# Mamba-2 block plus mixture of LoRA experts: B, half of h and the sums of squares turned by VectorE and DRAM instead of TensorE, with urgencies set unit by unit

## The chip, the cores and the metric

The kernel runs on one core of one Trainium2 chip. The metric is the device time of one execution in microseconds. Before the change the median of three runs is 1601.93 us (1601.57 to 1602.46). PE is TensorE's matmul, PEld its weight load, DVE VectorE, ACT ScalarE, POOL GpSimd, SP the engine that issues the DMAs.

## The reference

One token sequence of S = 1024 with 512 features is normalized, goes through a state-space layer (128 heads of 64 channels, state size 128, 8 groups, chunks of 128 tokens) and through a feed-forward part with routed low-rank experts, and both are added to the input. What matters here, cut:

```python
proj = jnp.einsum('bsd,ed->bse', x, in_proj_w)          # gate, h | B | C, dt
xc = jax.lax.conv_general_dilated(xc, conv_w, (1,), [(K - 1, 0)], ...)   # 4 taps per channel
hBC = jax.nn.silu(jnp.transpose(xc + conv_b, (0, 2, 1)))
...
xch = (hs * dt[..., None]).reshape(b, nc, CHUNK, H, P)
Y_diag = jnp.einsum('bzlhn,bzshn,bhzls,bzshp->bzlhp', Cc, Bc, L, xch)
states = jnp.einsum('bzlhn,bhzl,bzlhp->bzhpn', Bc, decay_states, xch)
Y_off = jnp.einsum('bzlhn,bzhpn,bhzl->bzlhp', Cc, prev, jnp.exp(A_cum))
Y = (Y_diag + Y_off).reshape(b, s, H, P) + hs * D[None, None, :, None]
g = y * jax.nn.silu(gate)
gg = g.reshape(b, s, G, INTER // G)
gg = gg * jax.lax.rsqrt(jnp.mean(gg * gg, axis=-1, keepdims=True) + EPS)
return jnp.einsum('bsi,oi->bso', gg.reshape(b, s, INTER) * norm_w, out_proj_w)
```

The convolution and the gate are computed with channels on the partitions and time along the free dimension. The sums over time (`states`, `Y_diag`) need h and B with time on the partitions, and the mean of squares needs a sum over channels for each time step. These are the places where data is turned.

## The kernel before

The inner 8192 channels are 64 blocks of 128 (two heads each); two blocks make a unit u of 0 to 31, four units make a group g of 0 to 7. All fp32 products are split into a high and a low fp32r part and done as three matmuls (hi x hi, hi x lo, lo x hi).

The kernel does not emit instructions as it goes. Each piece of work is registered with `op(engine, cost, function, reads, writes, urge=...)`, and `Plan.run` is a list scheduler. It goes through time with the costs written at the call sites, and on each engine starts the ready piece with the smallest urgency for which a buffer is free. For PE it adds a price from `URGE` when the shape of matmul changes: `SHORT` (transposes, cb), `LONG` (512 columns), `HALVES` (64 weight columns: yo and y), `MIDDLE` (ps). The result is a fixed order on each engine; on the chip every engine works through its order and waits on semaphores where data is not there. An `op` on SP that is a DMA has a `lag`, the time the plan allows until landing. `CAPS` bounds the buffers of each kind; buffers come from shared pools (`big`, `wide`, `small`, and `banks`, the 8 banks of PSUM).

The stages:

- Start: x is loaded in 8 parts, normalized, transposed on PE (`xT`) and split into `xh`, `xl`, both [features, time]. The time steps dt are projected and their cumulative sums go to DRAM (`acum_d`, `exp_d`), from where they are broadcast back as `L` and `e`.
- For each group, `group` makes B and C by `block`, the turned B as `bh` and `bl` (high and low part, time on the partitions), and `cbm`, the masked product of C and B. The turn before is 8 PE transposes into two PSUM banks (L718), read by ACT for `bh` (L720) and by DVE for `bl` (L722).
- `block` (L662 on) projects 128 channels: 2 x 12 matmuls of 512 columns into two banks (`pp_r`, L426), and for h, B and C the four taps of the convolution: one on ACT (L685), three on DVE (L694), then SiLU on ACT (L697).
- `scan(u, hs, gate)` does a unit: `L` (decays: ReLU and Exp on ACT, product with `cbm` on DVE, L762); `hT`, 8 PE transposes of h per block into PSUM (L776); `xdt`, turned h times dt, by two DVE instructions from PSUM (L778); `xf` on POOL, `xdh` on ACT and `xdl` on POOL; `ps`, the states' products (L802) and `st`, their recurrence on DVE; `yo` and `y` (L837, L849), their evacuations `tt` and `yt` on DVE, and the gated result on POOL, stored to DRAM (`g_d`).
- The feed-forward part (`ffn`) comes near the end of the scan.
- The output projection: for each group and each chunk z of 128 time steps `gr` is loaded from `g_d`, split into `gh` and `gl`, squared (ACT) and reduced over the group's 8 blocks into `sq` (DVE, L911), and 24 matmuls `po` (L920) run. For each four chunks PE transposes `sq` into `vp` (L932), DVE reduces it to one sum per time step (L934), and the reciprocal root scales `po` into `acc` (L941).

Of the kernel before, what the change touches and what calls it, by code (L numbers as in the profile page):

```python
# [49 lines left out]
URGE = dict(w=9.24, part=-0.279, proj=-0.002, evac=-1.876, silu=-2.632, group=-0.486, hT=0.407, xdt=2.385, xf=-1.176,  # L50
            split=-0.323, ps=-2.368, st=-1.089, Ll=-7.231, Lr=6.458, Le=2.863, Lm=5.964, el=-2.393, yo=0.086,
            tt=-1.918, y=3.42, yt=-3.901, out=1.039, switch=2.019, short=0.042, long=0.133, halves=-1.335,
            middle=-3.841, leave=2.869, c0=36.517, c=0.019, ffn=32.348, rt=-5.457, la=-0.436, early=-6.249,
            hold=0.232, gate=-0.092, w0=79.012)
CAPS = dict(hs=5, gate=15, ct=2, L=7, e=2, xdt=25, wr=3, wh=3, wl=8, y=4, tt=2, xf=2, mm=13, ts=3, yy=17)
# [42 lines left out]
class Plan:  # L98
# [33 lines left out]
    def run(self):  # L132
# [11 lines left out]
        while left:  # L144
            began = False
            soon = 1e30
            for e in ENGINES:
# [4 lines left out]
                for o in todo[e]:  # L152
                    same = e == "PE" and o.mode == mode == HALVES
                    if o.ready > t + 1e-9:
                        soon = min(soon, o.ready)
                        stay |= same and o.ready < t + URGE["hold"]
                        continue
# [3 lines left out]
                    if e == "PE" and o.mode != mode:  # L161
                        urge += URGE[("short", "long", "halves", "middle")[o.mode]]
                        if mode == HALVES:
                            urge += URGE["leave"]
# [10 lines left out]
                    for k, bs in wanted.items():  # L175
                        pool = k.pool
                        many[pool] = many.get(pool, 0) + len(bs)
                        if k.live + len(bs) > k.cap or (k.fifo and bs[0].order != k.given):
                            good = False
                            break  # L180
                        if k.late and pool.spare() < many[pool]:
                            good = False
                            break
                        ready = sorted(f[0] for f in pool.free)
                        if len(ready) < many[pool]:
                            good = False
                            break
                        if ready[many[pool] - 1] > t + 1e-9:
                            soon = min(soon, ready[many[pool] - 1])
                            stay |= same and ready[many[pool] - 1] < t + URGE["hold"]  # L190
                            good = False
                            break
# [50 lines left out]
def block_kernel(ctx, tc, x, in_w, conv_w, conv_b, dt_bias, A_log, Dv, norm_w, out_w,  # L243
# [30 lines left out]
    elast_d = dram.tile([H, NZ], F32, name="elast_d")  # L274
    g_d = [dram.tile([BPG, P, S], F32, name=f"g_d{g}") for g in range(G)]
# [5 lines left out]
    big, wide, small = Pool("big", 30, 1024, sb), Pool("wide", 3, 1792, sb), Pool("small", 15, 512, sb)  # L281
    K = {n: Kind(big, CAPS.get(n, 1)) for n in ("hs", "gate", "bT", "ct", "cbm", "bh", "bl", "L", "e", "xdt", "dts", "As",
# [6 lines left out]
    K |= {n: Kind(small, c, late=True) for n, c in dict(acc=8, sq=2, ow_r=4, moe=1, lb=1).items()}  # L289
# [11 lines left out]
    def thing(name):  # L301
        return pl.buf(None, name)

# [13 lines left out]
    XH, XL = new("xh", "xh", S, FR), new("xl", "xl", S, FR)  # L317
    G_D = [thing(f"g_d{g}") for g in range(G)]

    def dma(dst, src, lag, **kw):  # L320
        return op("SP", 0.45, lambda: sp.dma_start(dst(), src()), lag=lag, **kw)
# [15 lines left out]
    op("PE", 6.0, warm_up(12), w=[warm], urge=-9.0)  # L337
# [5 lines left out]
    for n, what in enumerate((0, 1, wdt, 2, 3, w0, 4, 5, 6, 7)):  # L343
        lag, urge = 2.64 + (0.3, 0.38)[n > 2] * n + 0.1 * (n > 2), -8.0 + 0.001 * n
        if what in (wdt, w0):
            dma(what[0], lambda row=144 if what is wdt else 0: in_w[row], lag, w=[what[0]], urge=urge)
        else:
            j, i = divmod(what, 2)
            dma(lambda j=j, i=i: xts[j]()[:, i, :], lambda z=what: x[zsl(z), :], lag, w=[(xts[j], 1 << i)], urge=urge)

    def load(*pairs):
# [5 lines left out]
    op("SP", 1.0, load((dtb, dt_bias), (negA, A_log)), w=[(CONST, 1)], urge=-7.9, lag=5.0)  # L357
    op("SP", 3.5, load((cw, conv_w), (cb, conv_b), (nw, norm_w), *(
        (Dt[64 * j:64 * j + 64, :], Dv[j:j + 1, :].partition_broadcast(64)) for j in range(2))), w=[(CONST, 2)],
       urge=2.5, lag=6.0)  # L360
    split(*wdt, -7.3)
# [45 lines left out]
    def project(w, acc, half, urge, take=(), quarters=False):  # L407

        for q in range(2) if quarters else ():
            def go(q=q):  # L410
                n, c = 0, slice(q * 256, q * 256 + 256)
                hi, lo = w[0](), w[1]()
                for a, b in ((hi, XH()), (hi, XL()), (lo, XH())):
                    for k in range(NK):
                        pe.matmul(acc()[:, c], a[:, k, :], b[:, k, halves(half)][:, c], start=n == 0, stop=n == 11)
                        n += 1
            mk = 3 << 4 * half + 2 * q
            op("PE", 1.44, go, r=[w[0], w[1], (XH, mk), (XL, mk)], w=[(acc, 1 << q)], urge=urge,
               take=take if q == 0 else (), mode=LONG)
# [244 lines left out]
    def block(u, i, row, ci, kind, name):  # L664
# [3 lines left out]
        if row:  # L668
            dma(raw, lambda: in_w[row], 3.6, w=[raw], urge=urge + URGE["w"])
# [35 lines left out]

    def group(g, u):
        gr = groups[g]
        urge = u + 0.16 + URGE["group"]
# [3 lines left out]
        for hf in range(2):  # L712
            zs = slice(hf * 4, hf * 4 + 4)
            acc = new("mm", f"bt{g}_{hf}", P)

            def turn(acc=acc, hf=hf):
                for z4 in range(4):
                    pe.transpose(acc()[:, z4, :], gr.B()[:, zsl(hf * 4 + z4)], ident)  # L718
            op("PE", 0.436, turn, r=[gr.B], w=[acc], urge=urge, take=[gr.bh, gr.bl] if not hf else ())
            op("ACT", 0.49, lambda acc=acc, zs=zs: act.activation(gr.bh()[:, zs, :], acc(), AF.Copy), r=[acc],  # L720
               w=[(gr.bh, zmask(hf))], urge=urge)
            op("DVE", 0.6, lambda acc=acc, zs=zs: dve.tensor_tensor(  # L722
                gr.bl()[:, zs, :], acc(), f32(gr.bh()[:, zs, :]), ALU.subtract), r=[acc, (gr.bh, zmask(hf))],
                w=[(gr.bl, zmask(hf))], urge=urge)
# [12 lines left out]


    def scan(u, hs, gate):
        g, gr = u // 4, groups[u // 4]  # L740

        def at(what):
            return u + URGE[what]
# [20 lines left out]
        for j in range(2):  # L764
            b = 2 * u + j
            cols = slice(j * P, (j + 1) * P)
            for hf in range(2):
                tp = new("ts", f"hT{b}_{hf}", P)
# [3 lines left out]
                late = 0.02 * (2 * j + hf)  # L772

                def turn(tp=tp, hf=hf, j=j):
                    for z4 in range(4):
                        pe.transpose(tp()[:, z4, :], hs[j]()[:, zsl(hf * 4 + z4)], ident)  # L776
                op("PE", 0.436, turn, r=[hs[j]], w=[tp], urge=at("hT") + late, take=[xdt[j]] if not hf else ())
                op("DVE", 0.6, lambda tp=tp, j=j, b=b, zs4=zs4: dve.tensor_tensor(  # L778
                    xdt[j]()[:, zs4, :].rearrange("p z (a c) -> p z a c", a=2),
                    tp().rearrange("p z (a c) -> p z a c", a=2),  # L780
                    dts()[:, zs4, 2 * b:2 * b + 2].unsqueeze(3).to_broadcast([P, 4, 2, 64]), ALU.mult),
                    r=[tp, dts], w=[(xdt[j], mk)], urge=at("xdt") + late)
# [11 lines left out]
        for i in range(4):  # L794
# [20 lines left out]
            op("DVE", sum(0.45 if z == 0 else 0.77 for z in zz), steps, r=[pt, eA], w=[(st, mk & 255)],  # L815
               urge=at("st") + 0.02 * i)
        for j in range(2):
# [6 lines left out]
            for hf in range(2):  # L824
                late = 0.04 * (2 * j + hf)
# [5 lines left out]
                def off(yo=yo, hf=hf, j=j):  # L831
# [7 lines left out]
                op("PE", 0.218 * n, off, r=[(st, 0x78 if hf else 7), gr.C], w=[yo], urge=at("yo") + late, take=[tt],  # L839
                   mode=HALVES)  # L840
# [4 lines left out]
                def diag(yp=yp, hf=hf, j=j):  # L845
# [6 lines left out]
                   urge=at("y") + late, take=[yt], mode=HALVES)  # L852
# [12 lines left out]
    def gates(u, base):  # L865
        return [block(base + URGE["gate"], 2 + j, 2 * u + j, None, "gate", f"g{2 * u + j}") for j in range(2)]

    first = [gates(u, URGE["early"] + 0.3 * u) for u in range(2)]
    for u in range(NU):
        if u % 4 == 0:  # L870
            group(u // 4, u)
        hs = [block(u, j, 64 + 2 * u + j, 2 * u + j, "hs", f"h{2 * u + j}") for j in range(2)]
# [6 lines left out]
    crs = ctile([P, 72], "crs")  # L879
    for g in range(G):  # L880
# [18 lines left out]
        for z in range(NZ):  # L899
# [24 lines left out]
            if z % many == many - 1:  # L924
                vp = new("ts", f"vp{g}_{z}", P)
                first = z - many + 1
                rs = crs[:, g * NZ + first:g * NZ + z + 1]
                RS = thing(f"rs{g}_{z}")

                def sums(vp=vp, sq=sq, many=many):  # L930
                    for j in range(many):
                        pe.transpose(vp()[:, j, :], sq()[:, j, :], ident)  # L932
                op("PE", 0.109 * many, sums, r=[sq], w=[vp], urge=urge + URGE["c"] - 0.1)
                op("DVE", 0.1 + 0.13 * many, lambda vp=vp, rs=rs, many=many: dve.tensor_reduce(  # L934
                    rs, vp()[:, 0:many, :], AX.X, ALU.add), r=[vp], w=[RS], urge=urge)
# [55 lines left out]
```

## Time and profile before

| what | value |
|---|---|
| median of three runs | 1601.93 us |
| the profiled execution | 1604.36 us |
| its span | 1602.7 us, 28828 instructions, granted TensorE clock 0.998 |
| VectorE, ScalarE and GpSimd busy | 1282.2, 1294.4 and 832.9 us |
| DMA | 229.98 MB, mean 143 GB/s |
| transposes of h / B / sums on PE | 512 / 64 / 64, 272 to 279 ns each (they overlap) |
| table loads on ACT | 203 by the instruction order, 1283 ns each |

The scan with its projections takes the time up to about 1240 us, and the output projection the rest. A group of instructions carries its line, its engine, its operation, its tile, the shapes, the count, the busy time in us, the mean duration in ns and the idle time of the engine just before. Matmul durations overlap, so spacing of starts tells more than duration.

### The profile page before, as it was taken

How to read it: one execution, taken by the hardware profiler on the slowest of the kernel's cores; microseconds unless marked ns; L12 is line 12 of the kernel's file. 1: busy time of each engine (PE TensorE's matmuls, PEld its weight loads, DVE VectorE, ACT ScalarE, POOL GpSimd, SP SyncE). 2: the span in 40 equal slices, each digit the busy share in tenths (PEclk: the TensorE clock that was granted, in tenths of full speed). 3: DMA queues.
4: the chain of work that ended last, by engine and by line, in shares of the span. 5: the costliest groups of instructions: out<-in, count | busy, mean ns of one | idle time of the engine just before them, and what ended most of it. 6: DMA issues, size and time to landing. Idle time of an engine off the chain costs nothing.

```text
span 1602.7 us, 28828 instructions
## 1 busy us (share of the span) xinstructions
PE 1592.1 (99%) x10616; PEld 1355.2 (85%) x10616; DVE 1282.2 (80%) x2209; ACT 1294.4 (81%) x2275; POOL 832.9 (52%) x768
## 2 busy tenths in 40 slices
PE   8999999999999999999999999999999999999999
PEld 8888888888888888888888888888887888888887
DVE  6798987786888788777878877787788788888874
ACT  6899989997999899799989988998973554444531
POOL 3269757847775776678576847866755000000000
PEclk9999999999999999999999999999999999999999
DMA  4534725444443555344344615544545655554512
GB/s 132 186 105 155 244 89 175 136 136 135 148 154 117 172 158 162 108 161 155 116 138 146 204 66 157 183 155 129 155 135 173 169 139 156 158 142 127 138 55 72
DMA packets 140605, 229.98 MB, mean 143 GB/s; under 512 B 11056, under 2 KB 76720, under 8 KB 140464
## 3 DMA queue, kind: packets, MB, share of 16 engines
q1 hardware_dynamic: 140464, 228.14, 46.5%
q8 instruction: 84, 1.38, 0.4%
q14 instruction: 57, 0.47, 0.1%
HBM read 191.39 MB, written 36.70 MB: 142 GB/s over the span
## 4 chain that ended last, share of the span: by engine, by line
PE 93%; POOL 3%; ACT 2%; issue 1%; DMA 0%; DVE 0%; SPq 0%; POOLq 0%; DVEq 0%
PE pp_r L426 45%; PE po L920 22%; PE y L849 7%; PE yo L837 6%; PE ps L802 5%; PE hT L776 3%; PE pf L652 1%; PE cb L732 1%; POOL yt L856 1%; POOL xdl L791 1%; POOL xf L784 1%; ACT L L758 1%; POOL g L859 1%; PE bt L718 0%; PE vp L932 0%
## 5 line engine op out<-in xcount | busy, mean ns | idle before, releaser
L426 PE MATMUL pp_r<-xh,wh 128*128 128x512 f32 x1144 | 454.2, 397 | 0.0
L426 PE MATMUL pp_r<-xh,wl 128*128 128x512 f32 x1144 | 446.3, 390 | 1.3 <-POOL wl L325 1.3
L426 PE MATMUL pp_r<-xl,wh 128*128 128x512 f32 x1144 | 446.4, 390 | 0.0
L694 DVE SCALAR_TENSOR_TENSOR h<-pp_r,cw,h 128x512 f32<-128x512 f32 (+2 forms) x384 | 283.3, 748 | 73.7 <-ACT h L685 67.7
L758 ACT ACTIVATE L<-L,As 128x128 f32<-128x128 f32 x1024 | 319.4, 391 | 0.0
L325 POOL TENSOR_TENSOR wl<-wr,wh 128x512 fp32r<-128x512 f32 x144 | 192.4, 1340 | 208.3 <-ACT wh L324 182.8
L426 PEld LDWEIGHTS pp_r<-xh,wl 128*128 128x128 f32 x1144 | 214.8, 188 | 48.3 <-POOL wl L325 2.2
L426 PEld LDWEIGHTS pp_r<-xh,wh 128*128 128x128 f32 x1144 | 215.0, 188 | 45.7 <-issue 3.9
L426 PEld LDWEIGHTS pp_r<-xl,wh 128*128 128x128 f32 x1144 | 215.2, 188 | 41.0
L762 DVE TENSOR_TENSOR L<-L,cbm 128x1024 f32<-128x1024 f32 x128 | 189.0, 1493 | 52.5 <-ACT L L760 52.1
L910 ACT ACTIVATE gr<-gr 128x1024 f32<-128x1024 f32 x64 | 67.8, 1060 | 157.6 <-DVE gl L908 157.6
L856 POOL TENSOR_TENSOR yt<-yt,tt 128x384 f32<-128x384 f32 (+1 forms) x128 | 157.3, 1240 | 68.8 <-DVE yt L853 60.4
L859 POOL TENSOR_TENSOR g<-yt,g 128x512 f32<-128x512 f32 x128 | 185.2, 1458 | 3.1
L791 POOL TENSOR_TENSOR xdl<-xf,xdh 128x512 fp32r<-128x512 f32 (+1 forms) x128 | 152.3, 1198 | 28.1 <-ACT xdh L789 28.1
L784 POOL TENSOR_TENSOR xf<-xdt,dec 128x512 f32<-128x512 f32 (+1 forms) x128 | 131.8, 1040 | 55.8 <-DVE xdt L778 55.6
L813 DVE SCALAR_TENSOR_TENSOR st<-st,eA,ps 128x64 f32<-128x64 f32 x768 | 151.4, 276 | 1.1
L911 DVE TENSOR_REDUCE sq<-gr 128x128 f32<-128x1024 f32 x64 | 128.7, 2013 | 19.1 <-ACT gr L910 19.0
L760 ACT ACTIVATE L<-L 128x1024 f32<-128x1024 f32 x128 | 135.6, 1059 | 1.5
L920 PE MATMUL po<-owh,gh 128*128 128x512 f32 x512 | 128.9, 394 | 0.0
L778 DVE TENSOR_TENSOR xdt<-hT,dts 128x512 f32<-128x512 f32 x128 | 80.2, 683 | 59.7 <-PE hT L776 59.7
L920 PE MATMUL po<-owh,gl 128*128 128x512 f32 x512 | 126.5, 389 | 0.0
L920 PE MATMUL po<-owl,gh 128*128 128x512 f32 x512 | 126.5, 389 | 0.0
(175 smaller groups left out, 2806.1 us busy)
## 6 DMA issues: line engine op xcount, KB each, us to landing
L<-acum_d SPq DMA_DIRECT2D x128, 512.0 KB, 5.8
wr<-in_w SPq DMA_DIRECT2D x144, 256.0 KB, 2.8
g_d<-g SPq DMA_DIRECT2D x64, 512.0 KB, 4.6
gr<-g_d SPq DMA_DIRECT2D x64, 512.0 KB, 6.7
e<-exp_d SPq DMA_DIRECT2D x128, 224.0 KB, 6.3
ow<-out_w SPq DMA_DIRECT2D x64, 256.0 KB, 3.6
x<-x SPq DMA_DIRECT2D x8, 256.0 KB, 5.3
acc<-x SPq DMA_DIRECT2D x8, 256.0 KB, 4.3
```

Source lines behind the costliest of these rows:

```text
L325: op("POOL", dur[1], lambda: pool.tensor_tensor(lo(), raw(), f32(hi()), ALU.subtract), r=[raw, hi], w=[lo], urge=urge, port=True)
L426: pe.matmul(acc(), a[:, k, :], b[:, k, halves(half)], start=n == 0, stop=n == 11)
L694: dve.scalar_tensor_tensor(d, acc()[:, :n], cw[:, ci, k:k + 1], d, ALU.mult, ALU.add)
L758: act.activation(L()[:, z, :], L()[:, z, :], AF.Relu, bias=As()[:, z, h:h + 1], scale=-1.0)
L760: op("ACT", 0.97, lambda L=L: act.activation(L(), L(), AF.Exp, scale=-1.0), w=[L], urge=at("Le") + 0.05 * a, table="exp")
L762: op("DVE", 1.14, lambda L=L: dve.tensor_tensor(L(), L(), gr.cbm(), ALU.mult), r=[gr.cbm], w=[L], urge=at("Lm") + 0.05 * a, port=True)
L784: op("POOL", 1.0 if n == 4 else 0.8, lambda xf=xf, j=j, b=b, zs=zs, n=n: pool.tensor_tensor(xf().rearrange("p z (a c) -> p z a c", a=2), x ...
L791: op("POOL", 1.24 if n == 4 else 0.96, lambda xf=xf, zs=zs, cols=cols: pool.tensor_tensor(xdl()[:, zs, cols], xf(), f32(xdh()[:, zs, cols] ...
L813: dve.scalar_tensor_tensor(st()[:, z, c], st()[:, z - 1, c], eA()[:, 4 * u + a, z:z + 1], pt()[:, z % 2, c], ALU.mult, ALU.add)
L856: op("POOL", 1.25 if n == 4 else 0.97, lambda yt=yt, tt=tt, part=part: pool.tensor_tensor(yt()[:, part], yt()[:, part], tt()[:, part], ALU ...
L859: op("POOL", 1.24, lambda yt=yt, j=j, hf=hf: pool.tensor_tensor(gate[j]()[:, halves(hf)], yt(), gate[j]()[:, halves(hf)], ALU.mult), r=[yt ...
L920: pe.matmul(po(), a()[:, b, :], wts[g, b // per][k]()[:, b % per, :], start=n == 0, stop=n == 23)
```

## The change

Three turns leave PE. A new function `turn` lets DVE turn each 32x32 square of a [128, 1024] tile in place of position (one instruction), stores the four quarters of it to DRAM (`turn_d`, four slots used in rotation) by four DMAs, and loads them back by one in such an order that whole 128x128 blocks come out transposed (`moved`). It is used for B of every group and for h of every second block (`TURNED = 2`: the odd ones); the even blocks keep `hT` on PE. `bh` and `bl` are then one instruction each, from SBUF; `xdt` of an odd block is two DVE instructions from `moved`, one per head. The sums of squares of a batch of four chunks are turned by 32x32 squares on DVE (`tq`), reduced to four partial sums per time step, stored by four DMAs in pieces of four numbers (`sums_d`), loaded back as 16 numbers per partition, and reduced again; the last group, with batches of two, keeps `vp` on PE.

The urgencies are all new, and `SHIFT` adds an own amount per unit and step for h, gate, group and every step of `scan`. The price of a change of matmul shape now depends on both shapes; an engine may now hold for any shape but `LONG`. The plan's landing times are scaled by `LAND = 1.15`. `big` has 33 buffers for 30, with 512 bytes of descriptor scratch instead of the default. At the start the loads of x and weights have another order, 13 warm-up matmuls stand for 12, and the 256-column projections wait part by part.

```diff
-CAPS = dict(hs=5, gate=15, ct=2, L=7, e=2, xdt=25, wr=3, wh=3, wl=8, y=4, tt=2, xf=2, mm=13, ts=3, yy=17)
+CAPS = dict(hs=5, gate=22, ct=2, L=7, e=2, xdt=17, turned=1, moved=2, wr=3, wh=3, wl=17, y=5, tt=3, xf=2, mm=30, ts=5, yy=4)
+SHIFT = {}
+for what, rows in dict(
+        Le={0: 0.93, 1: 0.09, 2: 0.4, 4: 0.59, 5: -0.15, 6: 2.11, 7: 0.07, 9: 1.91, 11: -2.72, 12: 2.6, 13: -0.73,
...
+    SHIFT |= {(u, what): by for u, by in rows.items()}
+LAND = 1.15
+TURNED = 2
+LATE_SUMS = True
...
-                        urge += URGE[("short", "long", "halves", "middle")[o.mode]]
-                        if mode == HALVES:
-                            urge += URGE["leave"]
+                        urge += URGE["SLHM"[mode] + "SLHM"[o.mode]]
...
+    turn_d = [dram.tile([4, 32, 4, 256], F32, name=f"turn_d{i}") for i in range(4)]
+    sums_d = [dram.tile([4, 32, 4, 4], F32, name=f"sums_d{i}") for i in range(4)]
...
+    def turn(src, name, at, urge):
+        turned, moved = new("turned", f"T{name}"), new("moved", f"M{name}")
+
+        def store():
+            for q in range(4):
+                sp.dma_start(turn_d[at][q].rearrange("r i f -> i r f"), turned()[:, 256 * q:256 * q + 256])
+        op("DVE", 1.17, lambda: dve.transpose(
+            turned().rearrange("p (q z c) -> p z q c", q=4, z=NZ), src().rearrange("p (z q r) -> p z q r", q=4, z=NZ)),
+            r=[src], w=[turned], urge=urge)
+        op("SP", 2.3, store, lag=LAND * 9.4, r=[turned], w=[TURN_D[at]], urge=urge)
+        dma(lambda: moved().rearrange("p (i f) -> p i f", i=4), lambda: turn_d[at].rearrange("q r i f -> (q r) i f"),
+            4.4, r=[TURN_D[at]], w=[moved], urge=urge)
+        return moved
...
-                op("PE", 0.436, turn, r=[hs[j]], w=[tp], urge=at("hT") + late, take=[xdt[j]] if not hf else ())
+            aside = TURNED and b % TURNED == TURNED - 1
+            if aside:
+                moved = turn(hs[j], f"h{b}", b % 4, at("hT"))
+                for a in range(2):
+                    op("DVE", 0.6, lambda j=j, a=a, h=2 * b + a, moved=moved: dve.tensor_tensor(
+                        xdt[j]()[:, :, 64 * a:64 * a + 64].rearrange("p z (i c) -> p z i c", i=2),
+                        flat4(moved).rearrange("p i (z c) -> p z i c", z=NZ)[:, :, 2 * a:2 * a + 2, :],
+                        dts()[:, :, h:h + 1].unsqueeze(2).to_broadcast([P, NZ, 2, 32]), ALU.mult),
+                        r=[moved, dts], w=[(xdt[j], ALL)], urge=at("xdt"), port=True)
...
+                if many == 4 and LATE_SUMS:
+                    tq, n = new("tq", f"tq{g}_{z}", P), 2 * g + z // 4
+                    QS = [thing(f"qs{i}") for i in range(2)]
+                    some, part = sums[:, 32 * n:32 * n + 16], sums[:, 32 * n + 16:32 * n + 32]
+                    op("DVE", 0.62, lambda tq=tq, sq=sq: dve.transpose(flat(tq), flat(sq)), r=[sq], w=[tq], urge=urge)
+                    op("DVE", 0.62, lambda tq=tq, some=some: dve.tensor_reduce(
+                        some.rearrange("p (b z) -> p z b", b=4), flat(tq).rearrange("p (z b c) -> p z b c", z=4, b=4),
+                        AX.X, ALU.add), r=[tq], w=[QS[0]], urge=urge)
+
+                    def store(some=some, at=n % 4):
+                        for i in range(4):
+                            sp.dma_start(sums_d[at][:, :, i, :].rearrange("b r z -> r b z"),
+                                         some[32 * i:32 * i + 32].rearrange("r (b z) -> r b z", b=4))
+                    op("SP", 1.9, store, lag=LAND * 6.0, r=[QS[0]], w=[SUMS_D[n % 4]], urge=urge)
+                    dma(lambda part=part: part, lambda at=n % 4: sums_d[at].rearrange("b r i z -> (b r) (i z)"), 3.0,
+                        r=[SUMS_D[n % 4]], w=[QS[1]], urge=urge)
+                    op("DVE", 0.15, lambda part=part, rs=rs: dve.tensor_reduce(
+                        rs, part.rearrange("p (i z) -> p z i", i=4), AX.X, ALU.add), r=[QS[1]], w=[RS], urge=urge)
...
-    nc = bacc.Bacc("TRN2", target_bir_lowering=False, num_devices=1)
+    nc = bacc.Bacc("TRN2", target_bir_lowering=False, num_devices=1, dynamic_dma_scratch_size=512)
```

## The prediction

> **What bounds the kernel now.** I read the page first: which engine is busy, and which one the chain of work that ended last runs through.
>
> ```profile
> PE 1592.1 (99%) x10616; PEld 1355.2 (85%) x10616; DVE 1282.2 (80%) x2209; ACT 1294.4 (81%) x2275; POOL 832.9 (52%) x768
> PE 93%; POOL 3%; ACT 2%; issue 1%; DMA 0%; DVE 0%; SPq 0%; POOLq 0%; DVEq 0%
> ```
>
> PE is busy in all but 10.6 of 1602.7 us and carries 93% of the chain. A mean over stages can mislead, so I next asked for two stretches: the scan (inner part) and the output projection. Columns: length, then busy us and instructions of PE, PEld, DVE, ACT, POOL, the granted clock, DMA share.
>
> ```profile
> 150.00:1150.00 1000.00, 998.77 (x7475) 865.05 (x7476) 805.59 (x1579) 946.14 (x1736) 703.54 (x634) 1.00 0.47 147
> 1250.00:1580.00 330.00, 330.00 (x1487) 273.07 (x1486) 271.82 (x263) 154.21 (x185) 0.00 (x0) 1.00 0.48 132
> ```
>
> PE is full in both, at full clock. DVE has 194 us free per 1000 in the scan and 58 of 330 in the output stage; ACT has only 54 per 1000 in the scan. So an instruction taken off PE shortens the program by its spacing, as long as the others follow. The spacing, not the duration, is the price, as matmuls overlap; the merged chain gives it (start, us, instructions).
>
> ```profile
> 683.33 1.75 PE hT L776 x16
> 685.08 10.92 PE pp_r L426 x48
> ...
> 1254.18 21.78 PE po L920 x96
> ```
>
> A transpose costs 1.75/16 = 0.109 us, a 512-column matmul 0.227. After a visit of transposes the next projection matmul starts some 0.08 us late and the visit begins 0.01 us late, but its first matmul follows early, so I take 0.110 all in.
>
> **What the change removes from PE.** h of 32 of 64 blocks: 32 x 8 = 256 transposes. B of 8 groups: 64. Sums of squares in 14 batches of four: 56. Together 376 x 0.110 = **41.4 us**. Nothing is put on PE (one warm-up more, before x is there).
>
> **What the new order adds on PE.** In the built instruction order the runs of 64-column matmuls (yo and y) are entered 55 times instead of 43, because urgencies differ by unit. A change of shape shows here (start, us):
>
> ```profile
> 415.37 1.04 PE L837 MATMUL yo<-C,st 128*64 128x128 f32 x16
> 416.34 0.50 PE L426 MATMUL pp_r<-xh,wh 128*128 128x512 f32 x1
> 416.68 0.40 PE L426 MATMUL pp_r<-xl,wh 128*128 128x512 f32 x1
> ```
>
> The two projection matmuls stand 0.34 apart, 0.11 above 0.227; entering costs 0.09 (0.32 from the last projection matmul at 409.32 to yo at 409.64). With the first yo's own lag I take 0.25 a visit, bounds 0.1 and 0.35: 12 x 0.25 = **+3.0 us** (1 to 4). Visits of transposes fall from 89 to 64, at 0.01 to 0.02 each: nothing.
>
> **What DVE gets.** No transpose on DVE is in this trace. Bounds per 1024 elements of a partition, SBUF to SBUF: the plain subtraction and the strided reduction.
>
> ```profile
> L908 DVE TENSOR_TENSOR gl<-gr,gh 128x1024 fp32r<-128x1024 f32 x64 | 78.8, 1232 | 0.0
> L911 DVE TENSOR_REDUCE sq<-gr 128x128 f32<-128x1024 f32 x64 | 128.7, 2013 | 19.1 <-ACT gr L910 19.0
> L934 DVE TENSOR_REDUCE crs<-vp 128x4 f32<-128x512 f32 x14 | 9.7, 692 | 16.7 <-PE vp L932 16.7
> ```
>
> I take 1.23 (one pass, as the first), upper 2.01. Scan: 40 turns x 1.23 = 49; xdt stays two instructions of 512 elements a block (0.68, now from SBUF); bl becomes 8 x 1.23 for 16 x 0.68, -1. So +48 us (upper 79) against some 137 left free: idle of 221 from 30 to 1200 us by the windows of that stretch, less 36 of the shortening, less 48. Output stage, per batch of four: a turn of 512 (0.62), a reduction (0.69), a small one (about 0.2, as the reciprocal's 0.17), less the old 0.69: +0.8 each, on 18.0 busy per 21.8 us (271.8/330); 3.0 stay free. DVE hides all of it at these prices; without that cover the same work would be 48 + 11 = 59 us.
>
> The Trainium skill speaks against this change (VectorE: DVE Perf Modes, Rules for kernel authors): a 128x128 transpose should go to TensorE where PSUM will do as its destination. The same page (The three transpose paths) gives 311 ns for a 128x128 bf16 turn on VectorE; an estimate from that is 8 x 0.311 = 2.5 us a turn and 100 instead of 49 us for DVE, still within its free time, so by the page the forecast would not move. The rule compares one instruction with another; this trace has PE full and DVE not.
>
> **ACT.** The built order has 174 table loads instead of 203; at 1.283 us each (the row of L760, 97 loads in 124.5 us) this frees 37 us, and 8 bh of 1.05 replace 16 of 0.58. ACT's share of the shorter scan stays near 95%. Without it, ACT would need 946 of 965 us and its waits would reach PE.
>
> **DMA and SP.** Each turn adds four stores of 128 KB and a load of 512 KB: 42 MB on 230, so the share of 46.5% goes to about 55%. The landings that bound the trip (KB, median us):
>
> ```profile
> wr<-in_w SPq DMA_DIRECT2D x144, 256.0 KB, 2.8
> g_d<-g SPq DMA_DIRECT2D x64, 512.0 KB, 4.6
> gr<-g_d SPq DMA_DIRECT2D x64, 512.0 KB, 6.7
> exp_d<-eT SPq DMA_DIRECT2D x1, 512.0 KB, 10.5
> ```
>
> Store 4.6 to 10.5, load 2.8 to 6.7: 7.4 to 17.2 us; I take 11.3 (g_d and gr, same size and route). SP issues the load of M in order, after waiting for the landing; up to 9 issues stand between the two, and in (weights) and L loads stand behind it. They are asked for several units (33 us each) before use.
>
> Two places can feel the trip. First DVE, in order, stands at xdt until M is there, and the taps that release PSUM stand behind. In the built order 10 to 35 us of DVE work, 20.5 in the mean, lie between a turn and its xdt (by the trace's durations); at 11.3 us only one turn of 40 is short, by 1 us. Second PE at ps. From the last projection matmul of the second block to the unit's first ps there are now 31 to 63 us of PE work (before 19 to 51, with hT on PE). The path: matmul 0.4, ACT 0.76, three taps 2.25, table load and SiLU 2.34, turn 1.23, trip 11.3, xdt 1.37, xf 1.06, xdh 0.62, xdl 1.35: 22.7 us, at the upper ends 29.4. It fits in every unit, with 8 us for queueing in the tightest (31.0).
>
> **Sums by DRAM.** The four stores move 16-byte pieces. The nearest rows are elast_d<-el (4 KB, 1.4) and dtb (0.5 KB, 4.9); the load, 2.4 to 6.7. Trip 3.8 to 11.6, I take 7. In the built order 7 to 11 us of DVE work, mostly near 8.5, cover it, and 3.0 a batch are free. The Trainium skill (DMA: Bandwidth & Descriptors) says that pieces under 512 B cost a read-modify-write; no row separates that out, and by it the trip would lie nearer its upper end.
>
> **Waits that remain.** Starts of matmuls more than 0.46 us apart sum to 9.5 us over the normal spacing, 3.3 of it before the first transpose of x. With DVE fuller and 54 more landings to wait for I add the other 6.2 once more, rounded to **+5 us**; bounds -6 (all of them gone) and +20 (ten units whose margin is under 3.5 us at the upper trip, 2 us each).
>
> **Sum.** Span 1602.7 - 41.4 + 3.0 + 5.0 = 1569.3. The profiled execution took 1604.36, 1.7 more than its span, and the median of the runs shown, 1601.93, lies 2.4 below it: 1569.3 + 1.7 - 2.4 = **1568.5 us**.
>
> **Rivals.**
> - Products come late (B): the trip at 17.2 and one foreign operation ahead on ACT, POOL and DVE (some 5 us) make the path 34.5; ten units have 31 to 34.4 us, together 20 us short: 1588. For it: ACT has 5% free. Against: 512 KB landed in 4.6 and 6.7 in the median.
> - The output stage waits for the sums (C, slower): DVE stands at the reduction of the returned sums, and acc, which frees the po banks, stands behind it. Cover and free time are 8.5 + 3.0 = 11.5 us; each us of trip beyond costs 14. From 13.9 us the gain is gone; at 15 us: 1568 + 14 x 3.5 = 1617. For it: gr loads of 6.7 us share the queues, and SP holds back the next gr meanwhile. Against: 1.4 us for the nearest small store.
> - DVE waits in the scan (D, slower): at a trip of 25 us the turns are short by 210 us in sum, 73 more than DVE has free: 1641; it decides from about 23.6 us.
> - Waits vanish with the finer urgencies (E): -6 instead of +5: 1557.5.
> - That the turn does nothing is excluded: 376 transposes are gone from PE's instructions.
>
> **Chances.** Forecast 0.67 (1560 to 1580), B 0.13, C 0.10, D 0.03, E 0.05, nothing gained 0.02. Time 1568; the range reaches from E to somewhat beyond B, 1557 to 1593, and leaves out C, D and a part of the rest. About 0.2% can be told from no change: faster 0.85, within 0.02, slower 0.13.
>
> **What would show it.** Right: PE's busy time down by 35 to 41 us at 98 to 99% share, 256 hT at unchanged spacing, DVE near 1340 us, turns near 1.2 us, M landing under 7 us. B: idle of PE before ps, ended by POOL xdl. C: PE under 97% after 1200 us, DVE idle before the reduction of sums, ended by a DMA. D: DVE idle before xdt, ended by M. The forecast is wrong if a turn takes over 2.5 us or a trip over 17.

## The result and the profile after

Median of 11 runs 1605.31 us (1603.18 to 1609.39), before 1602.46 us in 11 runs; ratio 1.0022, 95% interval 1.0013 to 1.0031. The change made the kernel slower by 0.2%, where 2% faster was forecast.

The page of the changed kernel, the lines that answer to those of before (busy time by engine, DMA queue, chain by engine and by line):

```profile
PE 1568.4 (98%) x10242; PEld 1320.5 (82%) x10242; DVE 1357.6 (85%) x2269; ACT 1257.5 (78%) x2238; POOL 858.5 (54%) x768
...
q1 hardware_dynamic: 177424, 270.32, 55.3%
...
PE 78%; DVE 6%; DMA 5%; ACT 5%; POOL 3%; issue 1%; SPq 0%; DVEq 0%; POOLq 0%; ACTq 0%
PE pp_r L494 35%; PE po L1013 22%; PE y L940 5%; PE yo L929 5%; PE ps L894 5%; DMA Mh<-turn_d 4%; DVE h L762 2%; ACT L L843 2%; PE pf L720 1%; PE hT L821 1%; POOL xf L876 1%; POOL xdl L883 1%; DVE xdt L856 1%; DMA wr<-in_w 1%; PE cb L813 1%
```

PE lost 374 matmuls, and its share of the chain fell from 93% to 78%. What came in is DMA, 5%, above all the load of the turned h, and the engines between that load and PE. The span did not shrink: PE now waits. The same stretches as before, and one more (length; busy PE, PEld, DVE, ACT, POOL; granted clock, DMA share, GB/s):

```profile
150.00:1150.00 1000.00, 980.53 (x7182) 836.70 (x7182) 868.43 (x1609) 907.94 (x1703) 725.83 (x630) 0.99 0.59 183
1250.00:1580.00 330.00, 330.00 (x1460) 273.09 (x1460) 285.19 (x300) 160.48 (x194) 0.00 (x0) 1.00 0.51 138
1195.00:1215.00 20.00, 15.67 (x104) 10.99 (x103) 14.61 (x33) 10.93 (x16) 9.02 (x8) 0.72 0.19 66
```

The output stage is full, as before. PE is 19.5 us idle in the scan (1.2 before), with gaps that the table below finds mostly at ps. DVE is not full there (868 of 1000), and ACT has become lighter. The query for the tile ps tells what those gaps waited for (us, times):

```profile
its engine sat idle before it (us, times) until:
  POOL xdl L883: 21.8, 19
  PE ps L894: 18.2, 13
  ACT xdh L881: 10.0, 10
```

The row `PE ps` is DVE waiting for ps; the other two are PE and its weight loads waiting for the parts of h. One such case, in the chain (start, us, what):

```profile
369.93 1.26 DVE Th L782
...
371.20 0.53 SPq L781
...
372.91 0.53 SPq L781
...
373.54 7.83 DMA Mh<-turn_d
...
381.39 0.69 DVE xdt L856
...
385.23 1.29 POOL xdl L883
...
386.56 1.46 PE ps L894 x10
```

The load of M whose own stores had landed at 369.66 us is issued only 3.9 us later, right behind the four stores of another block's turn, which come before it in SP's order, and lands 7.8 us after that. DVE, PE and POOL in that window:

```profile
377.60 1.23 DVE L847 TENSOR_TENSOR L<-L,cbm 128x1024 f32<-128x1024 f32 x1 [0.28 <-ACT L L845]
381.39 0.69 DVE L856 TENSOR_TENSOR xdt<-Mh,dts 128x512 f32<-128x512 f32 x1 [2.56 <-DMA Mh<-turn_d]
```
```profile
385.19 0.38 PE L894 MATMUL ps<-xdh,bh 128*128 128x256 f32 x1 [1.23 <-ACT xdh L881]
385.42 0.28 PE L894 MATMUL ps<-xdh,bl 128*128 128x256 f32 x1
386.56 0.38 PE L894 MATMUL ps<-xdl,bh 128*128 128x256 f32 x1 [0.87 <-POOL xdl L883]
```

DVE stands 2.56 us for M, the chain xdt, xf, xdh, xdl runs late, and PE, which works through its order, loses 1.23 and 0.87 us at ps. PE has no slack, so it never gets this back.

Where PE's time went, by the distance between starts of matmuls, summed by the tile of the later one (us; worked out from the traces; the last two columns are runs told of below: the changed order without h's stores and loads, and a new order that allows for later landings):

| tile | before | after | no trip | late, tuned |
|---|---|---|---|---|
| hT | 61.0 | 36.8 | 33.5 | 32.4 |
| bt and vp | 17.9 | 1.4 | 1.4 | 1.4 |
| ps | 85.4 | 106.7 | 86.2 | 95.5 |
| y and yo | 220.9 | 226.2 | 226.6 | 224.1 |
| pp_r and pp_rt, 512 columns | 781.4 | 789.7 | 789.3 | 784.2 |
| wp and we | 2.7 | 9.1 | 3.7 | 3.6 |

The transposes are gone (-40.7 with their gaps); ps took 21.3 back, the projections 8.3, wp and we 6.4, y and yo 5.3.

The landings of the DMAs issued between 150 and 1150 us (us from issue, median and three-quarter point), beside what the changed kernel's plan assumes. They are counted from the semaphores: in these traces a store of a turn adds five increments, every other DMA 16, and the counts come out even on every semaphore.

| load | before | after | no trip | assumed |
|---|---|---|---|---|
| weights wr | 2.75, 4.5 | 6.5, 7.3 | 3.4, 4.2 | 4.1 |
| L | 5.7, 7.2 | 7.5, 9.2 | 6.0, 7.1 | 6.9 |
| e | 6.5, 8.4 | 7.1, 8.5 | 4.8, 7.0 | 5.5 |
| M of h | - | 6.5, 9.3 | - | 5.1 |

The whole trip of h, from a turn's first store to the landing of M, takes 16.2 us in the median of the 32 blocks (11.3 to 23.9, a quarter of them over 19.7). 8.8 us of it pass until the four stores have landed, and the load is issued up to 6.4 us after that, as in the case above.

These stores stand out. The four of a turn are issued within 2.3 us and land 3.6, 5.2, 7.0 and 8.8 us after the first begins (medians). Where they alone are under way, little more than a quarter of the 16 DMA engines is busy (first row); with other loads under way it is most of them (second row; columns as above):

```profile
562.50:566.50 4.00, 4.00 (x19) 3.31 (x18) 4.00 (x7) 3.99 (x6) 2.57 (x3) 1.00 0.29 92
379.00:381.00 2.00, 2.00 (x12) 1.68 (x11) 0.00 (x0) 1.30 (x2) 0.00 (x0) 1.00 0.85 333
```

And the late weights are above all those beside such stores. Of 123 loads of weights, the 48 issued with a turn's store under way landed after 7.1 us in the median; the 32 beside a turn's load alone took 5.4, the other 43 took 3.5. With as many bytes under way (300 to 1200 KB) it is 7.1 us for 39 loads beside a turn's store and 3.1 to 3.6 for 22 beside other DMAs. This points to the form of these stores more than to the number of bytes, but no run changed the form alone.

### The profile page after: what moved, and what is told of

Read it like the earlier page. It is cut to its first block, busy times and chain, and to the rows that moved or that the text cites. A ratio compares the mean times of both kernels' runs of the same rounds, so it can differ in the third digit from the quotient of the medians.

```text
span 1602.5 us, 28531 instructions
## 1 busy us (share of the span) xinstructions
PE 1568.4 (98%) x10242; PEld 1320.5 (82%) x10242; DVE 1357.6 (85%) x2269; ACT 1257.5 (78%) x2238; POOL 858.5 (54%) x768
## 3 DMA queue, kind: packets, MB, share of 16 engines
q1 hardware_dynamic: 177424, 270.32, 55.3%
## 4 chain that ended last, share of the span: by engine, by line
PE 78%; DVE 6%; DMA 5%; ACT 5%; POOL 3%; issue 1%; SPq 0%; DVEq 0%; POOLq 0%; ACTq 0%
PE pp_r L494 35%; PE po L1013 22%; PE y L940 5%; PE yo L929 5%; PE ps L894 5%; DMA Mh<-turn_d 4%; DVE h L762 2%; ACT L L843 2%; PE pf L720 1%; PE hT L821 1%; POOL xf L876 1%; POOL xdl L883 1%; DVE xdt L856 1%; DMA wr<-in_w 1%; PE cb L813 1%
## 5 line engine op out<-in xcount | busy, mean ns | idle before, releaser
L876 POOL TENSOR_TENSOR xf<-xdt,dec 128x512 f32<-128x512 f32 (+1 forms) x128 | 140.5, 1111 | 113.5 <-DVE xdt L856 73.7
L883 POOL TENSOR_TENSOR xdl<-xf,xdh 128x512 fp32r<-128x512 f32 (+1 forms) x128 | 166.8, 1315 | 52.5 <-ACT xdh L881 51.9
L947 POOL TENSOR_TENSOR yt<-yt,tt 128x384 f32<-128x384 f32 (+1 forms) x128 | 161.4, 1270 | 47.8 <-DVE yt L944 36.7
L950 POOL TENSOR_TENSOR g<-yt,g 128x512 f32<-128x512 f32 x128 | 177.8, 1395 | 2.2
L905 DVE SCALAR_TENSOR_TENSOR st<-st,eA,ps 128x64 f32<-128x64 f32 x768 | 155.7, 275 | 2.2 <-PE ps L894 1.0
L940 PE MATMUL y<-L,xdt 128*64 128x128 f32 x2048 | 122.0, 274 | 1.6 <-DVE yt L944 1.1
```

Of the source, the lines that this page charges most:

```text
L876: op("POOL", 1.0 if n == 4 else 0.8, lambda xf=xf, j=j, b=b, zs=zs, n=n: pool.tensor_tensor(xf().rearrange("p z (a c) -> p z a c", a=2), x ...
L883: op("POOL", 1.24 if n == 4 else 0.96, lambda xf=xf, zs=zs, cols=cols: pool.tensor_tensor(xdl()[:, zs, cols], xf(), f32(xdh()[:, zs, cols] ...
L905: dve.scalar_tensor_tensor(st()[:, z, c], st()[:, z - 1, c], eA()[:, 4 * u + a, z:z + 1], pt()[:, z % 2, c], ALU.mult, ALU.add)
L940: pe.matmul(yp()[64 * a:64 * a + 64, zsl(z4)], xdt[j]()[:, z, 64 * a:64 * a + 64], M[2 * j + a]()[:, z, :], start=True, stop=True)
L947: op("POOL", 1.25 if n == 4 else 0.97, lambda yt=yt, tt=tt, part=part: pool.tensor_tensor(yt()[:, part], yt()[:, part], tt()[:, part], ALU ...
L950: op("POOL", 1.24, lambda yt=yt, j=j, hf=hf: pool.tensor_tensor(gate[j]()[:, halves(hf)], yt(), gate[j]()[:, halves(hf)], ALU.mult), r=[yt ...
```

## The experiments

**Take away the wait, then the traffic.** In the first run xdt of an odd block reads h itself, and all instructions and DMAs are still issued; in the second, stores and loads of h's trip are left out too. Each leaves out the turn of h of odd blocks.

```diff
-                        flat4(moved).rearrange("p i (z c) -> p z i c", z=NZ)[:, :, 2 * a:2 * a + 2, :],
+                        flat4(hs[j]).rearrange("p i (z c) -> p z i c", z=NZ)[:, :, 2 * a:2 * a + 2, :],
```


> The order of every engine is that of the changed kernel; xdt of an odd block reads h itself and not the h that came back from DRAM, so the turn of h of odd blocks is left out of the result. All its instructions and DMAs are still issued. Theory 1 (PE loses its 41 us to waits for the trip of h): 1605 less the 21 us that ps grew by and some 6 more behind it, 1570 to 1580. Rival 2 (the 42 MB of new traffic slow every landing, weights and decays too): 1592 or more, as only the wait is gone and not the traffic. Rival 3 (the new order itself is too tight for the engines, whatever the trip): above 1595.


```diff
-            for q in range(4):
+            for q in range(4 if name[0] == "B" else 0):
                 sp.dma_start(turn_d[at][q].rearrange("r i f -> i r f"), turned()[:, 256 * q:256 * q + 256])
...
+        def fetch():
+            if name[0] == "B":
+                sp.dma_start(moved().rearrange("p (i f) -> p i f", i=4), turn_d[at].rearrange("q r i f -> (q r) i f"))
```


> As the run without the wait, and the stores and loads of h to and from DRAM are not issued either (those of B and of the sums stay); the turn of h of odd blocks is left out of the result. Theory 1: within 5 us of the run without the wait, 1568 to 1580. Rival 2 (traffic): 1568 to 1580, but 12 us or more below the run without the wait, and in weights landing at 2.8 us again. Rival 3 (order): above 1595.

Measured 1584.73 us (ratio to before 0.9883, 0.9868 to 0.9898) and 1573.62 us (0.9816, 0.9799 to 0.9832). The first lies between what theory 1 and rival 2 expected, so both hold a part: of the 31.7 us between the changed kernel and the run without the trip, the wait for M takes 20.6, and 11.1 go with the stores and loads themselves. With these SP's five issues for each turn are gone as well, and its waits for them; traffic and SP were not separated. Without the trip PE no longer waits at ps; the two rows that stood at 21.8 and 10.0 us are gone:

```profile
its engine sat idle before it (us, times) until:
  PE ps L896: 18.8, 13
  ACT midT L685: 0.8, 1
  issue: 0.3, 2
  POOL xdl L885: 0.2, 1
```

The order of PE, DVE, ACT and POOL is the changed one, so rival 3 falls in this form: that order runs in 1573.6 us if its data come. The traffic shows in the table of landings: with h's trip out, the weights are back at 3.4 us.

A part of the 20.6 us came by way of the clock. In the changed kernel the granted clock stands at half in four stretches between 514 and 1218 us, 23.9 us in all, each at or right behind a gap of 1.8 to 4.3 us on PE, and 512-column matmuls start 0.427 us apart there instead of 0.228. Without the wait one such stretch of 6.8 us is left, behind a gap at wp. Counting the matmuls in them and their wider spacing, an estimate is 6 us of the 20.6.

**The descriptor scratch alone.**
```diff
-    nc = bacc.Bacc("TRN2", target_bir_lowering=False, num_devices=1)
+    nc = bacc.Bacc("TRN2", target_bir_lowering=False, num_devices=1, dynamic_dma_scratch_size=512)
```


> The kernel before with 512 bytes of descriptor scratch and nothing else. All theories: 1601 to 1604, landings of weights 2.8 us and of L 5.7 us as before. If the small scratch slows DMAs, landings grow and the time rises by 3 us or more.

1602.97 us, ratio 0.9997 (0.9988 to 1.0006): no part of it.

**The sums back on PE.**
```diff
-LATE_SUMS = True
+LATE_SUMS = False
```


> The changed kernel with the sums of squares turned on PE again, in the order that the plan makes of it. Theory 1: the trip of the sums costs nothing in the output stage (PE is busy all through there), so the 56 transposes come back: 1605 + 6 = 1611, between 1607 and 1614. Rival (the trip of the sums holds up the output stage): below 1603.

1614.19 us, ratio 1.0073 (1.0057 to 1.0088): 8.9 us more than the changed kernel, 0.2 above theory 1's range. By the spacing of starts the row of vp is 7.8 us higher (9.2 for 1.4), more than the 6.2 of 56 transposes at 0.110. The sums by way of DRAM gain; the rival of the output stage is wrong.

**SHIFT, and the landings that the plan assumes.** First SHIFT is left empty. Then the plan is also told later landings, taken from the changed kernel's trace at about the three-quarter point (M's 7.8 us lies below it: by the table above that is 9.3). Then h goes back to PE (without SHIFT, early landings).

```diff
-    SHIFT |= {(u, what): by for u, by in rows.items()}
+    pass
```


> The changed kernel without the amounts per unit (SHIFT empty); all else, the landing times that the plan assumes too, as changed. Theory 1 (the trip of h lands later than the order allows for, and its traffic delays the other loads): the loss is in this order as well, 1600 to 1615. Rival 3 (the urgencies by unit made an order that is too tight): 1595 or less.


```diff
-            4.4, r=[TURN_D[at]], w=[moved], urge=urge)
+            6.8, r=[TURN_D[at]], w=[moved], urge=urge)
...
-            dma(raw, lambda: in_w[row], 6.5 if row < 4 else 3.6, w=[raw], urge=urge + URGE["w"])
+            dma(raw, lambda: in_w[row], 6.5 if row < 4 else 6.4, w=[raw], urge=urge + URGE["w"])
...
-                lambda h=h: acum_d[h].partition_broadcast(P), 6.0, r=[ACUM_D], w=[L],
+                lambda h=h: acum_d[h].partition_broadcast(P), 8.0, r=[ACUM_D], w=[L],
```
(and so for e, 4.8 to 7.0, and g, 3.5 to 6.0)

> As the run without SHIFT, and the plan is told the landings that the trace of the changed kernel shows at its three-quarter point: M 7.8 us after its issue instead of 5.1, weights 7.4 instead of 4.1, L 9.2 instead of 6.9, e 8.1 instead of 5.5, g 6.9 instead of 4.0. So the order puts their users later. Theory 1: 20 us of waits and a part of the 11 us of traffic go, 1578 to 1592. Rival 2b (DMA time itself is short, so later users only move the waits): above 1598.


```diff
-TURNED = 2
+TURNED = 0
```


> The changed kernel without SHIFT and with h of all blocks turned on PE again; B and the sums still go by 32x32 turns and DRAM. From the run without the trip of h: 1573.6 + 256 x 0.110 = 1602, and some us more for the order without SHIFT: 1598 to 1608 by theory 1, so about the kernel before, and no worse than the changed kernel. Rival (the order of the new urgencies is what gains or loses): below 1592 or above 1612.

1624.6 us (ratio 1.0133, 1.0117 to 1.0148), 1608.08 (1.0039, 1.0027 to 1.0051) and 1606.2 (1.0021, 1.0012 to 1.0031). SHIFT gains 19 us; it is not what loses, and without it the loss is 10 us beyond what theory 1 expected. With urgencies unchanged, the later landings alone win 16.5 us, less than expected, and 1608 lies where rival 2b put it: the distances at ps fall from 122.8 to 95.4 us, but new gaps open elsewhere, where these urgencies do not fit the later landings (two of 4 and 6 us, before a run of hT and before wp). So this run left open whether an order can allow for the landings at all. h on PE without SHIFT runs as fast as the changed kernel, and 18.4 us faster than its like, the trip of h without SHIFT (1606.2 against 1624.6): with early landings the trip of h buys nothing, and in this order it loses.

**The urgencies searched anew.** Under the late landings, URGE, CAPS and SHIFT were changed at random in many small steps, and a step was kept where the plan did not become longer by it. A second order came of landings a fifth longer again, a third replaces the way through DRAM by 16 DMAs inside SBUF (there with assumed landings between the early and the late ones: 5.4, 7.0, 6.5 and 5.0 before the factor, for weights, L, e and g).

```diff
+URGE.update({...})
+CAPS.update({...})
+SHIFT.clear()
...
+    SHIFT |= {(u, what): by for u, by in rows.items()}
```


> The landings of the run with the late plan, and the urgencies searched anew in the plan under these landings (it had been the changed kernel's urgencies without SHIFT, 1608). The traffic is all there. Theory 1 (an order that allows for the landings does not wait): 1573.6 of the run without the trip plus the 11 us of traffic that no order removes, 1576 to 1592. Rival 2b (DMA time is short in itself): above 1598.


```diff
-FREE = 0.17
+FREE = 0.25
...
-LAND = 1.15
+LAND = 1.4
```
(and a projection's second half of 256 columns waits for its first)

> As the late plan, with all landing times taken a fifth longer still (LAND 1.4 for 1.15) and buffers handed on 0.08 us later, urgencies searched anew. Theory 1: if what is left of the loss is landings at the upper end (a tenth of the L loads take over 10 us, of e over 12), this order is the better one, 1574 to 1588 and below the run before it; if the traffic itself costs, both are alike.


```diff
+            for q in range(4):
+                for i in range(4):
+                    sp.dma_start(moved()[32 * q:32 * q + 32, 256 * i:256 * i + 256],
+                                 turned()[32 * i:32 * i + 32, 256 * q:256 * q + 256])
+        op("SP", 8.5, move, lag=LAND * 11.0, r=[turned], w=[moved], urge=urge)
```


> B and h of odd blocks go from the turned tile to the moved one by 16 DMAs inside SBUF (each 32 partitions of 1 KB), with no store to DRAM and no load, so 21 MB less are moved and no landing of a store is waited for; urgencies searched anew in the plan. The result is the reference's. Theory 1: half of the 11 us of traffic gone and one landing for two: 1572 to 1588. Rival (issuing is the cost: 16 issues of about 0.5 us occupy SP for 8 us a turn, 330 us in all, and hold up the loads behind): above 1595.

**1574.52 us** (ratio 0.983, 0.9815 to 0.9845), 1575.65 (0.9836, 0.9822 to 0.9851) and 1619.08 (1.0097, 1.0073 to 1.012). The first beats both kernels, with all the traffic there. Its page:

```profile
PE 1554.8 (99%) x10242; PEld 1316.7 (84%) x10242; DVE 1345.1 (86%) x2269; ACT 1242.5 (79%) x2226; POOL 866.5 (55%) x768
...
q1 hardware_dynamic: 177424, 270.32, 57.0%
```

The same packets and bytes, and landings as late as in the changed kernel (weights 6.7, L 7.8, M 7.8, e 8.3 us in the median). So an order that allows for them gets back what the late landings cost, as far as the run without the trip shows it (1573.6), and rival 2b falls. That does not make the trip free: an order searched without it was not run, and the second control below leaves 13 us open. More margin (1575.65) wins nothing more. The way inside SBUF misses its range and lies where its rival was expected: one piece of 32 KB lands in 1.9 us, and the 16 of a turn in 12.1 from the first issue, but their issues take 10.8 us on SP in the median, where the plan allowed 8.5, and the run lost 40 us and more against the way through DRAM. That points to SP's issuing; it was not tried apart, and the assumed landings differ too.

**Two controls.** The same search, as long, under the early landings; and the late landings with h on PE.

> Control of the tuned run with the late plan: the same start, the same search for as long, but under the landings that the changed kernel's plan assumes (M 5.1, weights 4.1, L 6.9, e 5.5, g 4.0 us). If the assumed landings are what loses the time (theory 1): 1592 to 1612, 18 us or more above the late one's 1574.5. If it was a better search (rival): 1570 to 1582.

> h of all blocks turned on PE, B and sums by 32x32 turns, the late landings, urgencies searched as long. Theory 1: with an order that allows for the landings the trip of h is worth its 256 transposes: 1574.5 + 28 = 1602 less what the lighter traffic spares, 1590 to 1602. Rival (the trip of h gains nothing even in a good order, as it fills DVE and DMA): 1582 or less.

1618.7 us (ratio 1.0103, 1.0088 to 1.0118) and 1589.72 us (0.9924, 0.9908 to 0.9941). The search alone is no help: 44 us lie between the two searched orders, which differ in the landings that the plan assumed. Each is the outcome of one search; the order with more margin is a second one under late landings, and agrees within 1.2 us. What PE (and DVE, in the row `PE ps`) waited for at ps, first under the early landings, then under the late ones:

```profile
its engine sat idle before it (us, times) until:
  POOL xdl L907: 38.4, 40
  ACT xdh L905: 26.5, 18
  PE ps L918: 14.4, 13
```
```profile
its engine sat idle before it (us, times) until:
  PE ps L918: 17.6, 14
  POOL xdl L907: 7.9, 13
  ACT xdh L905: 6.0, 6
```

And the turn of h is worth 15 us (1589.7 to 1574.5) of the 28 that its 256 transposes cost. Most of the other 13 stands at ps, 95.5 us by the spacing of starts with the trip and 85.9 with h on PE. Under the early landings, without SHIFT, the turn of h had cost 18.4 us.

## Why the prediction was wrong

**Right.** PE was the bound, and its removed work was sized well: in the run without the trip hT, bt and vp are 44.0 us lower, 41.4 forecast; 2.6 of the 44.0 come back in the row of the projections, where the first two matmuls behind a visit of transposes take 0.34 us together and not 0.46, and such visits are fewer now. A turn on DVE takes 1.24 us (1.23); the 2.5 us estimated from the bf16 figure of the Trainium skill (VectorE: DVE Perf Modes, The three transpose paths) were not seen. ACT fell by 37 us (37), the DMA share rose to 55.3% (55). The sums' trip, which by the Trainium skill (DMA: Bandwidth & Descriptors, Specifications: a read-modify-write below 512 B) was at risk, costs nothing that PE feels, and the two slower rivals (C in the output stage, D by DVE alone) did not happen: PE is full after 1250 us, and DVE waits for M 27.4 us in all:

```profile
DVE xdt L856 <- DMA Mh<-turn_d: 27.4, 10, 5.1
```

**A term too small.** The visits of yo and y: +3.0. In the run without the trip y, yo and the 512-column projections stand 13.6 us higher. By the spacing of starts 5.0 of it are single waits longer than 0.46 us, 2.6 the projections that no longer start early, mostly behind transposes, 1.5 matmuls at half clock, and 4.3 the visits: 2.4 for the entries and 1.8 for 22 more returns straight to 512-column matmuls, which the sum had not counted by themselves. So the size was near; the waits belong to the next term.

**The step that failed.** "It fits in every unit, with 8 us for queueing in the tightest (31.0)", and with it "+5 us" for the waits that remain. Two things stood behind it. The trip was taken at 11.3 us from two medians of before; it took 16.2 in the median, and 13 of 32 trips took more than the upper end of 17.2. The store had been sized at 4.6 after g_d, a store of 512 KB in one DMA; the four stores of a turn, 512 KB together, took 8.8. The load's own issue waited on SP for up to 6.4 us more, and the load alone took up to 11.9. And all other landings were left as they were: the 42 MB were charged to the queues' share (46.5 to 55%), and nothing to the latency of the loads that stand beside them, though the weights' median went from 2.75 to 6.5 us. The runs put 20.6 us on the first, and 11.1 on the second together with SP's work for the trip; the forecast without both, 1568.5, is 5 us from the 1573.6 measured without the trip. Rival B named the place (ps, behind xdl), and its sign is there, with 20 us and a chance of 0.13, but as the worst case of one load.

The deeper reason lies in the kernel's own text, and the prediction passed by it. An order made by a plan holds the landings that the plan assumes. The kernel before assumed 3.6 us for weights that landed in 2.75. The changed one assumed 4.1 and got 6.5. For the whole trip of h it allowed 15.9 us (10.8 for the stores, 5.1 for the load), already 4.6 more than the prediction's 11.3, and this was met only by about half of the trips. I measured DVE's and PE's cover against my own estimate of the path, unit by unit, and not whether the assumed times hold under the new load.

What stays open: how much of the 44 us belongs to M, to the weights and to L each; the late plan changed them together. Whether stores in a form that keeps more DMA engines busy would shorten the trip and spare the weights. And whether fewer issues, in one hop, would do better than the way through DRAM.

## What to carry to other kernels

Where an order is fixed ahead from assumed times, check each assumed landing against the trace with the change's own traffic in it, before anything else; a saturated engine cannot make up for a late arrival, and here one arrival delayed a chain of four engines. To tell a wait from its traffic, let the consumer read something that is already there, first with the DMAs still issued and then without them; the second step takes the issuing engine's work out too. Size a transfer from one of the same form and not only of the same bytes. Here the change was sound and the assumed landings were not: with later ones, near the measured, and the order searched again, the same change is 1.7% faster than before.

## What the hardware showed beyond that

- A mean share says little of a load's latency: 256 KB of weights went from 2.75 to 6.5 us in the median while the DMA engines' mean share rose only from 46.5% to 55.3%; without h's trip, at 48.9%, it was 3.4. The late ones stood beside the stores of a turn (7.1 us, against 3.5 with no DMA of a turn beside them).
- A single gap on PE cost twice. After 4.3 us of idling before wp, at 1201 us, the granted clock is 0.72 in the mean of the 20 us around it (third row of the first windows above), and the four matmuls `we` that follow are 0.85 us apart instead of 0.43 before.
- Sixteen-byte pieces to DRAM, 7168 of them, did no harm that a run shows.
